# Inverting a Sinkhorn chain's sums on ScalarE (logarithm, exponential) or on VectorE (reciprocal)

## The chip, the cores and the metric

The kernel runs on one core of a Trainium2 chip. Its time is the device time of one execution in microseconds (us). An engine works through its own queue of instructions strictly in order; the queues meet through semaphores.

## The reference

Two layers work on two batches of 1024 rows of 512 numbers. The first layer is a single-head attention and, behind it, a mixing of four streams per row by a 4x4 matrix. The second layer is an attention with 32 heads, followed by a gated sum of low-rank experts. The edit lies in the mixing: the 4x4 matrix of a row comes from 50 Sinkhorn steps, each of which normalizes first the rows and then the columns.

```python
Z = logits / tau                                   # tau = 0.1
def step(carry, _):
    u, v = carry
    u = -jax.nn.logsumexp(Z + v[..., None, :], axis=-1)
    v = -jax.nn.logsumexp(Z + u[..., :, None], axis=-2)
    return ((u, v), None)
(u, v), _ = jax.lax.scan(step, (u0, v0), None, length=50)
H_res = jnp.exp(Z + u[..., :, None] + v[..., None, :])
...
H_res = (1.0 - g) * I + g * H_res
x_mixed = jnp.einsum('btij,btjc->btic', H_res, x_streams)
```

## The kernel before

**Sinkhorn.** A batch's 1024 matrices lie as 128 partitions x 8 x 4 x 4, so one instruction works on all of them: 128 elements per partition for a matrix (tiles M, Kt, Z), 32 for the row sums (aa) or column sums (bb). All of these tiles bear the name sk in the profile. The first step is made with logarithms (L535 to L549); the other 49 are made on the exponentials: `chain_pool` for the second batch, `chain_dve` for the first. In `chain_pool` GpSimd multiplies the matrix by the inverse sums (L567, L573) and adds it up in two instructions (L568 and L569 for the rows, L574 and L575 for the columns), and VectorE inverts the 32 sums (L572, L577). So one iteration crosses between the engines four times. At iteration 25 the factors are taken into Z once (L579 and after).

**What sets the order.** The chain is a Python generator. One `next` issues half an iteration: 102 of them are spread over 116 slots of the second layer (SK0, SKN, `chain_step`). A slot is one row step of the second layer's attention; there are 512. Which instruction stands where in an engine's queue is decided at build time by a scheduler with a model of the engines' times, from the program's order and the dependences. An edit of one instruction can thus move others in the queues.

**The row step** (`row_step`) computes a block of scores on TensorE (L91 into tile s), takes the row minimum on VectorE (L292, L296), the exponential with its sum on ScalarE (L300), the inverse of the sum (L324 on VectorE, L325 on ScalarE), the upper half in 16 bits on ScalarE (L330) and the lower on VectorE (L338). The columns up to a multiple of 128 are cleared on GpSimd (L342). Then SyncE's queue issues the transpose by DMA (L343), and TensorE multiplies with the values (L373) some slots later. Heads come in groups of four, 32 slots per group; a row is finished one slot after its scores.

**The other work in these slots:** weights come in by DMA on GpSimd's queue (L715) and are split there into two halves (L97 to L99; L97 waits by hand for a step of VectorE, L338). ScalarE and VectorE evacuate products (L107, L108), VectorE adds to the result (L775). The gating of the experts runs on VectorE (L921 to L961, with L204 and L205 on ScalarE). After the chain its result Hm mixes the second batch's streams (`mix0_units`, L635 loads xr on SyncE's queue, L659 on ScalarE, L660 on GpSimd), from slot 122 on.

Of the kernel before, what the change touches and what calls it, by code (L numbers as in the profile page):

```python
# [11 lines left out]
AF = mybir.ActivationFunctionType  # L12
# [42 lines left out]
def tile_model(ctx: ExitStack, tc: tile.TileContext, out: bass.AP, a: dict):  # L55
# [3 lines left out]
    V, A, G = nc.vector, nc.scalar, nc.gpsimd  # L59
# [497 lines left out]
    def chain_pool(b, Z, M, aa, bb, over_i, over_j, f2):  # L557

        Kt = sk[b, 1].rearrange("p t (i j) -> p t i j", j=4)
        h2 = sk[b, 5].rearrange("p t (i j) -> p t i j", j=2)  # L560
        h3 = h2.rearrange("p t i j -> p t (i j)").rearrange("p t (k j) -> p t k j", k=2)
        A.activation(Kt, Z, AF.Exp)
        x = Kt
        yield
        for it in range(1, 50):
            if x is not Kt:
                G.tensor_tensor(M, Kt, over_i(bb), ALU.mult)  # L567
            G.tensor_tensor(h2, x[:, :, :, 0:2], x[:, :, :, 2:4], ALU.add)  # L568
            G.tensor_tensor(aa, h2[:, :, :, 0], h2[:, :, :, 1], ALU.add)  # L569
            x = M  # L570
            yield
            V.reciprocal(aa, aa)  # L572
            G.tensor_tensor(f2(M), f2(Kt), over_j(aa), ALU.mult)  # L573
            G.tensor_tensor(h3, x[:, :, 0:2, :], x[:, :, 2:4, :], ALU.add)  # L574
            G.tensor_tensor(bb, h3[:, :, 0, :], h3[:, :, 1, :], ALU.add)  # L575
            yield
            V.reciprocal(bb, bb)  # L577
            if it == 25:
                A.activation(aa, aa, AF.Ln)  # L579
                A.activation(bb, bb, AF.Ln)  # L580
                V.tensor_tensor(f2(Z), f2(Z), over_j(aa), ALU.add)
                V.tensor_tensor(Z, Z, over_i(bb), ALU.add)
                A.activation(Kt, Z, AF.Exp)
                x = Kt
        V.tensor_tensor(M, M, over_i(bb), ALU.mult)
# [643 lines left out]
```

## Time and profile before

| what | value |
|---|---|
| time, median of 3 runs | 1848.05 us (1846.22 to 1849.40) |
| the profiled execution's own time | 1850.09 us |
| its span | 1848.3 us |
| mean granted clock of TensorE | 0.973 of full speed |
| TensorE busy, share of the span | 1710.0 us, 93% |
| VectorE | 1475.5 us, 80% |
| ScalarE | 1189.3 us, 64% |
| GpSimd | 868.0 us, 47% |
| the chain's stretch (first L568 to last L577) | 276.3 to 593.2 us |

The page names the engines PE (matmul) and PEld (weight load) for TensorE, DVE for VectorE, ACT for ScalarE, POOL for GpSimd and SP for SyncE; SPq and POOLq are instructions that issue DMAs. L572 is line 572 of the kernel. A line of waits reads: engine, tile and line that waited, behind the arrow the engine, tile and line that ended the wait, then the total in us, how often, and the longest. A line of the timeline reads: start and duration in us, engine, line, operation, tiles and shape, count, and in brackets the idle time before it with what ended that. In a table by stretch the columns are the stretch, its length and each engine's busy time with its count of instructions, then the granted clock, the DMA engines' share and what they moved. Matmuls overlap, so that a busy TensorE is not one at its peak: in the chain of work that ended last, twelve matmuls of 512 columns take 2.59 us, 0.216 us each, while the page's mean of one is 0.380.

### The profile page before, as it was taken

What the parts mean: (1) busy time and instruction counts of PE and PEld (TensorE: products, weight loads), DVE (VectorE), ACT (ScalarE), POOL (GpSimd) and SP (SyncE); (2) the same over time, 40 slices, a digit from 0 to 9 for tenths busy, and PEclk for the clock granted to TensorE, in tenths of its full rate; (3) what the DMA queues carried; (4) which work ended last, traced back from release to release, by engine and by line L of the source; (5) the groups of instructions that cost most, each with busy time, mean ns of one, the idle gap of its engine ahead of it and who ended that gap; (6) DMA issues with size and microseconds to landing.
All of it is one profiled execution on the core that took longest, in us unless ns stands there. A gap on an engine that the chain in (4) does not pass through costs nothing. (4 is left out here: it accounts for less than half of the span.)

```text
span 1848.3 us, 35002 instructions
## 1 busy us (share of the span) xinstructions
PE 1710.0 (93%) x11394; PEld 1040.1 (56%) x11394; DVE 1475.5 (80%) x4170; ACT 1189.3 (64%) x2917; POOL 868.0 (47%) x1460
## 2 busy tenths in 40 slices
PE   4767399899999999998999999999999999999998
PEld 2434156555666556665565566665666666665565
DVE  7888878978888878777577777799787877778676
ACT  3848666656676777876366666667566767666564
POOL 5568639766867455656244242334142423235200
PEclk9888699999999999999999999999999999999999
DMA  7435216666566656476383655557565655666455
GB/s 212 83 55 131 60 44 140 139 107 139 120 139 114 137 125 141 103 149 139 71 170 96 128 123 132 101 137 164 146 142 119 141 125 132 128 143 127 103 118 117
DMA packets 685033, 228.14 MB, mean 123 GB/s; under 512 B 665633, under 2 KB 665761, under 8 KB 684850
## 3 DMA queue, kind: packets, MB, share of 16 engines
q1 hardware_dynamic: 669394, 178.65, 47.1%
q0 software_dynamic: 13152, 43.07, 8.2%
q10 hardware_dynamic: 2304, 4.20, 0.7%
q8 instruction: 89, 1.46, 0.3%
q14 instruction: 94, 0.77, 0.1%
HBM read 52.81 MB, written 4.19 MB: 31 GB/s over the span
## 5 line engine op out<-in xcount | busy, mean ns | idle before, releaser
L300 ACT ACTIVATE P<-P,nm 128x1024 f32<-128x1024 f32 (+31 forms) x528 | 391.4, 742 | 279.9 <-DVE nm L292 256.0
L338 DVE SCALAR_TENSOR_TENSOR Phl<-P,r,Phl 128x64 f16<-128x64 f32 (+16 forms) x627 | 461.1, 760 | 77.6 <-ACT Phl L330 71.4
L91 PE MATMUL s<-K,Q 128*128 128x512 f16 (+22 forms) x2400 | 441.2, 317 | 19.0 <-DVE P L296 11.2
L373 PE MATMUL av<-PT,V 128*128 128x256 f16 x3456 | 427.6, 275 | 13.1 <-DMA PT<-Phl 11.0
L373 PEld LDWEIGHTS <-V 128*128 128x128 f16 x3456 | 339.3, 99 | 97.1 <-issue 11.6
L330 ACT ACTIVATE Phl<-P,r 128x1024 f16<-128x1024 f32 (+31 forms) x515 | 369.7, 731 | 17.1 <-DMA PT<-Phl 2.9
L91 PE MATMUL pp<-wo,ao 128*128 128x512 f16 x1536 | 369.3, 380 | 5.6 <-ACT ao L107 3.1
L91 PE MATMUL pp<-big,wq 128*128 128x512 f16 x1536 | 368.6, 380 | 2.0 <-DVE Q L108 1.9
L97 POOL TENSOR_SCALAR f2k<-f2k 128x512 f32<-128x512 f32 x164 | 111.2, 679 | 520.0 <-DVE Phl L338 467.7
L91 PEld LDWEIGHTS <-Q 128*128 128x128 f16 x2400 | 224.1, 98 | 177.4 <-issue 28.5
L91 PEld LDWEIGHTS <-wq 128*128 128x128 f16 x1536 | 148.8, 98 | 167.9 <-DVE Q L108 2.4
L91 PEld LDWEIGHTS <-ao 128*128 128x128 f16 x1536 | 149.7, 98 | 161.9 <-ACT ao L107 4.9
L91 PEld LDWEIGHTS <-big 128*128 128x128 f16 x1824 | 121.2, 100 | 86.4 <-DMA big<-wo 40.7
L292 DVE CUSTOM_DVE_ANT_0 P<-s,mask,nm 128x272 f32<-128x272 f32 (+15 forms) x256 | 157.7, 617 | 11.3 <-PE s L91 3.0
L296 DVE TENSOR_SCALAR_CACHE_REDUCE P<-s 128x512 f32<-128x512 f32 (+15 forms) x272 | 152.6, 563 | 10.7 <-PE s L91 9.3
L325 ACT ACTIVATE r<-r 128x1 f32<-128x1 f32 x528 | 95.9, 193 | 76.7 <-DVE r L324 76.1
L324 DVE RECIPROCAL r<-r 128x1 f32<-128x1 f32 x528 | 79.9, 156 | 81.5 <-ACT P L300 78.2
L342 POOL MEMSET Phl<- 128x192 f16 (+1 forms) x320 | 56.3, 188 | 162.6 <-DMA PT<-Phl 99.3
L107 ACT ACTIVATE ao<-av 128x512 f16<-128x512 f32 x128 | 75.0, 586 | 87.4 <-PE av L373 84.0
L292 DVE CUSTOM_DVE_ANT_0 P<-s,mask 128x32 f32<-128x32 f32 (+15 forms) x256 | 104.6, 430 | 19.2 <-PE s L91 18.9
L91 PE MATMUL pp<-big,big 128*128 128x128 f16 (+2 forms) x816 | 103.9, 283 | 16.8 <-DVE sk L604 12.7
L775 DVE SCALAR_TENSOR_TENSOR acc<-pp,acc 128x512 f32<-128x512 f32 x128 | 87.2, 681 | 36.7 <-PE pp L91 36.3
(257 smaller groups left out, 2064.2 us busy)
## 6 DMA issues: line engine op xcount, KB each, us to landing
f2k<-in_Wq POOLq DMA_DIRECT2D x64, 256.0 KB, 3.2
f2k<-in_WoT POOLq DMA_DIRECT2D x64, 256.0 KB, 3.2
PT<-Phl SPq DMA_TRANSPOSE x528, 3.3
acc<-in_x SPq DMA_DIRECT2D x16, 256.0 KB, 5.2
f2k<-in_Wup POOLq DMA_DIRECT2D x16, 256.0 KB, 3.3
xr<-V SPq DMA_DIRECT2D x32, 128.0 KB, 2.3
out<-acc ACTq DMA_DIRECT2D x16, 256.0 KB, 3.0
xr<-in_x SPq DMA_DIRECT2D x12, 256.0 KB, 3.6
```

The lines of the kernel that those rows point to most:

```text
L91: nc.tensor.matmul(dst, lhs(l), rhs(r), start=(i == 0 and j == 0), stop=(i == n - 1 and j == 2))
L97: first = G.tensor_scalar(stage, stage, scale, 1.0, ALU.mult, ALU.mult)
L107: A.activation(hl_hi, src, AF.Copy, scale=scale)
L292: last_row[0] = V.tensor_tensor_reduce(Pm[:, o:o + w], pt[:, :w], mask[:, 512 - w:], -scale, first, ALU.add, ALU.min, nm[:, k:k + 1])
L296: last_row[0] = V.tensor_scalar(Pm[:, o:o + w], pt[:, :w], -scale, first, ALU.mult, ALU.min, accum_out=nm[:, k:k + 1])
L300: A.activation(Pm[:, :W], Pm[:, :W], AF.Exp, bias=last, scale=-1.0, accum_out=r[:, 0:1])
L324: V.reciprocal(r[:, 1:2], r[:, 0:1])
L325: A.activation(r[:, 1:2], r[:, 1:2], AF.Copy, scale=PSCALE)
L330: A.activation(hl[1], Pm[:, :W], AF.Copy, scale=r[:, 1:2])
L338: last_low[0] = V.scalar_tensor_tensor(lo, Pm[:, a0:a1], r[:, 1:2], hi[:, a0:a1], ALU.mult, ALU.subtract)
L373: nc.tensor.matmul(p, v, pt, start=(k == 0), stop=(k == len(todo) - 1))
L775: V.scalar_tensor_tensor(acc[b, t], p, 1.0 / 256.0, acc[b, t], ALU.mult, ALU.add)
```

## The change

The two calls of the reciprocal in `chain_pool` become calls of a helper. Up to iteration 45 it takes the logarithm of the sums in place on ScalarE and then the exponential of its negative; from iteration 46 on it is the reciprocal on VectorE as before. `chain_dve` is not touched.

```diff
         A.activation(Kt, Z, AF.Exp)
         x = Kt
+
+        def inverse(s):
+            if it < 46:
+                A.activation(s, s, AF.Ln)
+                A.activation(s, s, AF.Exp, scale=-1.0)
+            else:
+                V.reciprocal(s, s)
+
         yield
         for it in range(1, 50):
@@
-            V.reciprocal(aa, aa)
+            inverse(aa)
             G.tensor_tensor(f2(M), f2(Kt), over_j(aa), ALU.mult)
@@
-            V.reciprocal(bb, bb)
+            inverse(bb)
```

In the changed kernel the lines behind the helper stand 8 lower: its logarithm is L559, its exponential L560, its reciprocal L562.

## The prediction

> **What bounds the kernel now.** I read the page's first and second parts, then the busy table of the stretch in which the edited code runs, then the waits of TensorE in that stretch, then those of GpSimd, and last the instructions of the tile sk.
>
> The second batch's Sinkhorn chain (tile sk, L567 to L577) runs from 276 to 593 us of a span of 1848.3 us. Beside it TensorE works on the first groups of layer 1's attention. Busy time there, in two pieces:
>
> ```profile
> core 0: us, PE busy (x) PEld busy (x) DVE busy (x) ACT busy (x) POOL busy (x), PEclk, DMA share, GB/s
> 276.00:376.00 100.00, 89.92 (x661) 55.88 (x660) 89.80 (x257) 60.59 (x151) 81.74 (x148) 0.96 0.69 139
> 376.00:593.00 217.00, 215.84 (x1439) 133.26 (x1438) 180.82 (x517) 141.56 (x348) 157.40 (x362) 0.99 0.60 124
> ```
>
> TensorE stands still for 10.1 us of the first 100 us and for 1.2 us of the 217 after. So nothing can be won after 376, only lost; what can be won lies before. VectorE is 90% busy in the first piece, ScalarE 61%. What ended TensorE's pauses between 276 and 593:
>
> ```profile
> PE av L373 <- DMA PT<-Phl: 5.5, 1, 5.5
> PE s L91 <- DVE P L296: 2.6, 1, 2.6
> PE av L373 <- DVE ao L108: 1.3, 1, 1.3
> PE pp L91 <- ACT ao L107: 1.2, 1, 1.2
> PE s L91 <- DVE nm L292: 0.6, 1, 0.6
> ```
>
> Three of five end with VectorE (4.5 us together), and the largest ends with a DMA that VectorE feeds. Next, who keeps GpSimd waiting in the same stretch, and the edited instructions beside the nearest logarithm:
>
> ```profile
> POOL sk L567 <- DVE sk L577: 20.3, 27, 2.0
> POOL f2k L97 <- DVE Phl L338: 19.5, 12, 5.7
> POOL sk L573 <- DVE sk L572: 16.2, 23, 2.8
> ```
> ```profile
> L572 DVE RECIPROCAL sk<-sk x49: 327/347/354, 277.9 to 591.6; 128x32 f32<-128x32 f32 x49
> L577 DVE RECIPROCAL sk<-sk x49: 326/349/355, 286.3 to 593.2; 128x32 f32<-128x32 f32 x49
> L542 ACT ACTIVATE sk<-sk x2: 213/221/229, 43.4 to 269.4; 128x32 f32<-128x32 f32 x2
> ```
>
> GpSimd asks for an inverse 98 times and pauses for many of the answers; with the pauses behind L324 (4.6 and 3.9 us) and L207 (0.8) they make 45.8 us.
>
> **What the change takes away.** 90 of the 98 reciprocals (iterations 1 to 45, two each) leave VectorE: 90 x 0.347 = 31.2 us. VectorE's own pauses for GpSimd in front of them (L572 8.3 us, L577 7.2 us) go too, but for the last four iterations.
>
> What that is worth is read from where TensorE stands still. Between the pauses at 276, 291.9, 339.7, 357.4 and 373.2 us the trace has 2, 10, 5 and 5 reciprocals, or 0.66, 3.46, 1.69 and 1.70 us. Against the pauses: of 1.30 us (ao, L108) 0.66 goes; of 2.60 us (P, L296) all; of 0.60 us (nm, L292) all. Sum **3.9 us**. From below, nothing goes if what VectorE waits for is late next: the rows that L338 needs come from ScalarE.
>
> The largest pause needs its own reading. TensorE's queue in front of it, SyncE's queue, and the landing times of the transposes between 358 and 374:
>
> ```profile
> 361.36 2.78 PE L373 MATMUL av<-PT,V 128*128 128x256 f16 x24
> ...
> 373.15 5.26 PE L373 MATMUL av<-PT,V 128*128 128x256 f16 x24 [5.46 <-DMA PT<-Phl]
> ```
> ```profile
> 363.17 0.33 SPq L635 DMA_DIRECT2D xr<-in_x  x1
> 364.52 2.24 SPq L343 DMA_TRANSPOSE PT<-Phl  x1
> ```
> ```profile
> DMA to landing us min/median/max: 2.8/6.1/8.6
> ```
>
> The transpose issued at 364.52 lands 8.6 us later, just ahead of TensorE's start at 373.15; over the chain's stretch the median landing is 3.4 us. It goes out right behind the 256 KB load of xr (L635), which had waited 2.1 us for VectorE's gating step L934. After the pause the same 24 matmuls take 5.26 us where the earlier 24 took 2.78, at a granted clock of 0.50 between 372 and 376: 2.48 us more. So this place costs 5.46 + 2.48 = 7.94 us. In the instruction order that the changed kernel is built with, the gating comes earlier on VectorE (its last L934 stands ahead of the lower half of the 992-wide row, not behind it) and xr's load stands one transpose earlier on SyncE. That takes the load out of the way of the late transpose. From above 7.94 us, from below nothing, since the loads of Wq on GpSimd's queue crowd the same moment. I take half, **4.0 us**.
>
> **What it adds.** 180 ScalarE instructions on 128x32. Logarithm: the row above, 0.22 us. An exponential of that shape is not in the trace; it lies between the copy of 128x1 (L325, 0.193) and the exponential of 128x128 (L540, 0.293 to 0.309), nearest the logarithm: 0.22. Sum 90 x 0.44 = 39.6 us on ScalarE, 202.2 us busy of 317 before, 241.8 after (76%). That fits beside its work: ScalarE's longest idle times there are waits for VectorE (L300 for nm, 71.6 us), which get shorter.
>
> The gating's Ln and Exp (L204, L205) run at 1207.60 and 1207.84 us for 0.21 each with nothing between them, and the one table load of the trace is at L110; in the changed order there is again one. The Trainium skill ("ScalarE: Activation LUTs", What ACT_TABLE_LOAD costs) puts a switch to another set of functions at 2.66 us, which would make 180 x 2.66 = 479 us if the two functions lay apart; its section on table sets names one set with both, and the trace agrees.
>
> The cost that can reach TensorE is GpSimd's. It sits 0.47 us between its two instructions when VectorE answers at once (0.35 of it the reciprocal). On ScalarE that is 0.47 - 0.35 + 0.22 + 0.09 (the gap between L325 and a dependent L330) + 0.22 = 0.65, so 0.18 more; x 90 = **16 us** at the least. In the changed order 43 of the 90 exponentials have another ScalarE instruction between them and their logarithm, mostly L300 or L330 (means 0.742 and 0.731 us): 43 x 0.74 = 32 more, **48 us** at the most. How long the request lies in the queue changes little: VectorE began 0.78 us (aa) and 0.41 us (bb) after the sum on average, and ScalarE begins L325 0.59 us after the L324 it waits for (all from start times in the timeline).
>
> Of the whole answer time before (49 x 1.44 + 47 x 1.02 = 118 us) 45.8 us, 39%, stood as idle time on GpSimd; the rest lay beside its other work. So 6 to 19 us more idle time, middle 12.5. It meets 19.5 us of slack, the waits of L97 for VectorE, but these lie at 12 places. What is queued behind a waiting GpSimd is the clearing of pad columns (L342), for which SyncE's transposes wait, and behind these TensorE's L373. There the order leaves room: a row is finished in the next slot, slot 4c+2 for the later row of a pair, its product is due in slot 4c+5, a slot is some 3.1 us (1572 us for 512), so 9.2 less 3.4 for the landing, nearly 6 us. I let a quarter of the middle through: **3.1 us**.
>
> Behind a waiting logarithm stand ScalarE's exponentials (L300) and evacuations (L107); VectorE paused 15.5 us for the same sums, and ScalarE has 75 us left, so I cost that at nothing; with the slack gone it is 15.5 us.
>
> The chain's end moves by some three rows in the changed order (about 10 us). The next to need it is mix0 (L659), first at 624 us, 31 us behind the chain's end: covered. From about 690 us on TensorE's order is the same in both kernels.
>
> GpSimd's L574 takes 318 ns by the median and 1204 at the longest, the long ones beside VectorE's L338. The Trainium skill ("SBUF — State Buffer", Who interferes with whom) says that a VectorE instruction with two SBUF inputs blocks a GpSimd instruction that reads SBUF, and that one with a single input in the plain mode doesn't. A reciprocal has one, so by this rule its leaving frees nothing there; the sum has no such gain either.
>
> **Sum.** The profiled execution took 1850.09 us (span 1848.3 and 1.79 around it). -3.9 - 4.0 + 3.1 = -4.8, so 1845.3. The median of the three runs shown, 1848.05, is 2.04 lower; on that footing **1843.3**, I write 1843.
>
> **Rivals.**
> - *The pauses only move.* The late transpose stays late (the Wq loads crowd it) and ScalarE's added work eats the rest: -3.9 + 3.1 = -0.8, 1847. For it: the DMA share is 0.69 there already. Against: the load of xr does move. 0.21.
> - *Slower: GpSimd becomes the bound.* The 48 us fall on it whole. It is busy 239 us of 317, pauses 46, issues 32 fetches at 0.59 us (19 us): only the 19.5 us are left. 48 - 19.5 - 6 (room of the transposes) = 22 us, less the 3.9 that VectorE gives: 1848 + 18 = 1866. It decides once GpSimd idles (19.5 + 6) / 90 = 0.28 us more per inverse, against 0.14 in the forecast. Half of that excess makes 1857. For it: GpSimd's order is strict and SyncE's transposes already wait for GpSimd in some 75 places. Against: the changed order puts other work between. 0.32.
> - *It doesn't do what it says:* table loads between the two functions, at the trace's 1.28 us a load 180 x 1.28 = 231 us. Excluded by the one load in the built order; 0.01.
> - *Forecast*, both gains in some measure: 1836 (all 11.8 us of the early pauses, nothing lost) to 1844. 0.46.
>
> **How the numbers follow.** 0.2% is 3.7 us, about what a measurement of this kernel can tell from no change. The forecast's case gives faster, the first rival same, the second and third slower: 0.46, 0.21, 0.33. The range leaves out little below (1834, a further 2 us of pauses behind 640 us) and the slower rival's far part: up to 1861.
>
> **What would show it.** Right: VectorE's busy time between 276 and 593 falls by some 31 us, ScalarE's rises by some 40; TensorE's pauses at 340 and 373 us shrink; L97's waits shrink. Wrong: pauses of TensorE (L373 for PT) after 376 us; GpSimd's waits for the exponential well over 58 us in all; TensorE's matmul of layer 1 at the same place of its order later from 420 us on.

## The result and the profile after

The changed kernel takes 1856.72 us (median of 6, 1855.54 to 1859.63) where the kernel before took 1848.17 in runs beside it: a ratio of 1.0038, 95% interval 1.002 to 1.0056. It is slower: the medians lie 8.6 us apart, and the ratio on record, which is not the quotient of the two medians, makes it some 7 us. On another chip the same kernel came out at 1.0014 (1.0003 to 1.0026). Both intervals lie above 1, so the sign is firm; the size is not. The profiled execution took 1855.54 us, span 1853.8, at a granted clock of 0.972 (before: 0.973), 5.5 us more than the one before.

In the profile of the changed kernel the logarithm is L567, the exponential L568 and the helper's reciprocal L570 (not the numbers that stand under the diff above). Lines behind the helper are 8 higher than before: GpSimd multiplies in L575 and L581 and sums in L576, L577 (rows) and L582, L583 (columns).

First the instructions of the tile sk in the changed kernel (shortest, median and longest in ns, then when):

```profile
L567 ACT ACTIVATE sk<-sk x90: 212/229/231, 279.6 to 594.1; 128x32 f32<-128x32 f32 x90
L568 ACT ACTIVATE sk<-sk x90: 212/229/231, 281.0 to 594.3; 128x32 f32<-128x32 f32 x90
```

The change does what it says, at the price that was estimated (0.22 us each). The eight reciprocals that stay on VectorE follow until 611.0 us, 18 later than the chain's last one before. Busy time by stretch, the changed kernel; the second stretch reaches to 603 us here:

```profile
core 0: us, PE busy (x) PEld busy (x) DVE busy (x) ACT busy (x) POOL busy (x), PEclk, DMA share, GB/s
276.00:376.00 100.00, 92.56 (x677) 57.30 (x675) 88.36 (x240) 66.25 (x189) 77.97 (x138) 0.95 0.67 136
376.00:603.00 227.00, 220.75 (x1461) 135.48 (x1459) 165.45 (x449) 164.71 (x500) 159.68 (x365) 0.99 0.58 121
```

The second stretch of the kernel before, to the same moment:

```profile
376.00:603.00 227.00, 225.84 (x1503) 139.58 (x1502) 188.24 (x541) 147.07 (x359) 160.44 (x368) 1.00 0.58 121
```

The kernel before has 278.0 us of VectorE and 207.7 of ScalarE in the same 327 us, this one 253.8 and 231.0. VectorE is relieved by 24 us and ScalarE takes on 23: less than the durations say (31 and 40), because neighbours on an engine overlap. In the fence on place 3 below, the exponential of 0.23 us at 453.00 is followed by an instruction that starts 0.13 later.

Now the waits between 276 and 600 us, of GpSimd, ScalarE and VectorE in the changed kernel, and behind them those of ScalarE and VectorE before:

```profile
POOL sk L581 <- ACT sk L568: 31.5, 28, 3.1
POOL sk L575 <- ACT sk L568: 28.5, 27, 2.9
POOL f2k L97 <- DVE Phl L338: 10.8, 8, 2.2
```
```profile
ACT sk L567 <- POOL sk L583: 28.0, 27, 2.3
ACT P L300 <- DVE nm L292: 26.9, 25, 6.5
ACT sk L567 <- POOL sk L577: 16.0, 19, 2.2
```
```profile
DVE r L324 <- ACT P L300: 25.2, 36, 1.8
DVE Phl L338 <- ACT Phl L330: 15.1, 23, 2.1
```
```profile
ACT P L300 <- DVE nm L292: 75.5, 51, 4.7
```
```profile
DVE r L324 <- ACT P L300: 9.6, 18, 1.0
DVE Phl L338 <- ACT Phl L330: 8.4, 15, 1.2
DVE sk L572 <- POOL sk L569: 8.3, 15, 1.8
DVE sk L577 <- POOL sk L575: 7.4, 15, 0.8
```

GpSimd waits 60.0 us for ScalarE's inverses, and 3.0 more for VectorE's last eight by the chain's end, where it waited 45.8 in all. ScalarE now waits 44.0 us for GpSimd's sums, and 48.6 us less than before for the row minimum (75.5 there). VectorE is rid of its own 15.7 us of waits for the sums, but waits 40.3 us for ScalarE's exponential and upper half where it waited 18.0. So 24 us of work and 15.7 us of waits left VectorE, and 22.3 us of waits for ScalarE came back.

TensorE's three longest pauses between 276 and 600 us, in the changed kernel's timeline:

```profile
296.16 2.08 PE L373 MATMUL av<-PT,V 128*128 128x256 f16 x9 [4.27 <-DVE ao L108]
...
457.66 0.62 PE L91 MATMUL s<-K,Q 128*128 128x160 f16 x6 [1.92 <-DVE nm L292]
469.69 4.06 PE L373 MATMUL av<-PT,V 128*128 128x256 f16 x24 [3.00 <-DMA PT<-Phl]
```

The first was 1.30 us before; the last two were not there, though before TensorE paused 1.16 us for ao (L107) at 459.1. The 2.60 us at 340 have shrunk to 0.27, the 5.46 us at 373 are gone, the 0.60 us at 357 are 0.71, and 1.58 us for ao (L107) are new at 361.7.

To see where the time moved, compare the start of each row's exponential (L300, in the timeline of ScalarE) with that of the same row in the profile before. From the first row of the stretch to the last of the kernel the difference is made of five parts:

| rows (time before) | difference gained or lost | what lies there |
|---|---|---|
| up to row 24 (274 us) | +0.6 | ahead of the edited work |
| 24 to 32 (to 294 us), **place 1** | +3.7 | the pause of 4.27 |
| 56 to 64 (371 to 401 us), **place 2** | -7.2 | the late transpose, gone |
| 80 to 168 (459 to 710 us), **place 3** | +6.3 | the pauses of 1.92 and 3.00, and slower matmuls behind |
| the other rows | +2.1 | small waits for L107 (in all 3.4 us, 1.2 before) |

The sum is +5.5, what the span shows. From 710 us on the two kernels keep their distance within about 1 us (+5.1 there, +5.5 at the end). The parts are not pauses alone: between the two rows of place 3 TensorE stands still 2.98 us before and 6.09 after, which is half of the 6.3. The other half is time in which it is busy; its granted clock between 376 and 603 us is 0.99 where it was 1.00.

### The profile page after: what moved, and what is told of

The parts are those of the page before. It is cut to its first block, busy times and chain, and to the rows that moved or that the text cites. A ratio compares the mean times of both kernels' runs of the same rounds, so it can differ in the third digit from the quotient of the medians.

```text
span 1853.8 us, 35062 instructions
## 1 busy us (share of the span) xinstructions
PE 1711.5 (92%) x11394; PEld 1039.0 (56%) x11394; DVE 1451.8 (78%) x4080; ACT 1214.9 (66%) x3097; POOL 871.6 (47%) x1460
## 5 line engine op out<-in xcount | busy, mean ns | idle before, releaser
L300 ACT ACTIVATE P<-P,nm 128x1024 f32<-128x1024 f32 (+31 forms) x528 | 391.0, 741 | 236.3 <-DVE nm L292 222.8
L338 DVE SCALAR_TENSOR_TENSOR Phl<-P,r,Phl 128x64 f16<-128x64 f32 (+16 forms) x627 | 458.7, 756 | 93.6 <-ACT Phl L330 78.6
L373 PE MATMUL av<-PT,V 128*128 128x256 f16 x3456 | 428.2, 276 | 16.2 <-DMA PT<-Phl 10.8
L373 PEld LDWEIGHTS <-V 128*128 128x128 f16 x3456 | 339.1, 99 | 100.0 <-DMA PT<-Phl 12.9
L97 POOL TENSOR_SCALAR f2k<-f2k 128x512 f32<-128x512 f32 x164 | 110.8, 677 | 501.7 <-DVE Phl L338 448.2
L292 DVE CUSTOM_DVE_ANT_0 P<-s,mask,nm 128x272 f32<-128x272 f32 (+15 forms) x256 | 158.3, 619 | 9.3 <-PE s L91 1.0
L324 DVE RECIPROCAL r<-r 128x1 f32<-128x1 f32 x528 | 80.5, 157 | 96.2 <-ACT P L300 93.1
L325 ACT ACTIVATE r<-r 128x1 f32<-128x1 f32 x528 | 96.1, 192 | 59.7 <-DVE r L324 57.4
L107 ACT ACTIVATE ao<-av 128x512 f16<-128x512 f32 x128 | 75.0, 586 | 81.4 <-PE av L373 78.1
L292 DVE CUSTOM_DVE_ANT_0 P<-s,mask 128x32 f32<-128x32 f32 (+15 forms) x256 | 104.4, 431 | 23.7 <-PE s L91 23.3
L91 PE MATMUL pp<-big,big 128*128 128x128 f16 (+2 forms) x816 | 103.8, 282 | 17.2 <-DMA big<-wo 16.7
```

The costliest lines, as they stand in the source:

```text
L91: nc.tensor.matmul(dst, lhs(l), rhs(r), start=(i == 0 and j == 0), stop=(i == n - 1 and j == 2))
L97: first = G.tensor_scalar(stage, stage, scale, 1.0, ALU.mult, ALU.mult)
L107: A.activation(hl_hi, src, AF.Copy, scale=scale)
L292: last_row[0] = V.tensor_tensor_reduce(Pm[:, o:o + w], pt[:, :w], mask[:, 512 - w:], -scale, first, ALU.add, ALU.min, nm[:, k:k + 1])
L300: A.activation(Pm[:, :W], Pm[:, :W], AF.Exp, bias=last, scale=-1.0, accum_out=r[:, 0:1])
L324: V.reciprocal(r[:, 1:2], r[:, 0:1])
```

## The experiments

**Theory:** the change's cost is made at a few places where an engine that works strictly in order stands still for another, not evenly over 90 inversions. **Rivals:** each inversion costs alike; or ScalarE's added load costs; or what counts is only that the build makes another order. Each run is compared with the kernel before on the same chip (1850.9 to 1851.5 us there). The table has every run; the differences at the places are taken as above, from one profiled execution each. Executions of one kernel scatter: those of place go from 1850.6 to 1858.2 us, and up to row 24, ahead of the edited work, the profiled ones differ from that of the kernel before by -2.4 to +3.2 us. The parts at the places repeat better (place 1 is 0.0 or +3.7 in 13 of the 16 runs), but each is one execution, while the medians come from all (12 of a kernel in most cases, 6 of skip112).

| run | ScalarE inverts in iterations | place 1 | place 2 | place 3 | median us | ratio (95% interval) |
|---|---|---|---|---|---|---|
| after_again | 1-45 (the change) | +3.7 | -7.2 | +6.5 | 1854.90 | 1.0014 (1.0003 to 1.0026) |
| none | nobody, 1-45 | +5.5 | -8.3 | +2.3 | 1850.80 | 0.9998 (0.9985 to 1.0011) |
| dummy | none | 0.0 | -0.4 | +0.1 | 1852.75 | 1.0015 (1.0001 to 1.0028) |
| load | none | +1.2 | -5.8 | +0.3 | 1848.62 | 0.9988 (0.998 to 0.9997) |
| wait | none | +0.1 | -5.8 | +4.8 | 1854.17 | 1.0014 (1.0001 to 1.0026) |
| mid | 4-19 | 0.0 | -7.0 | +1.7 | 1850.08 | 0.9992 (0.998 to 1.0004) |
| from4 | 4-45 | 0.0 | -7.0 | +3.6 | 1852.19 | 1.0005 (0.9995 to 1.0016) |
| hole | 1-19, 26-45 | +3.7 | -7.2 | +3.7 | 1853.62 | 1.0009 (0.9997 to 1.0021) |
| place | 20-25 | +3.7 | -1.0 | +4.5 | 1853.13 | 1.0014 (1.0002 to 1.0026) |
| skip | 4-19, 26-45 | 0.0 | -7.0 | 0.0 | 1842.70 | **0.9957 (0.9944 to 0.997)** |
| before120 | none, 120 slots | 0.0 | 0.0 | -0.2 | 1849.21 | 0.9992 (0.9979 to 1.0005) |
| after120 | 1-45, 120 slots | +3.7 | -7.2 | +3.2 | 1852.39 | 0.9999 (0.9989 to 1.0009) |
| before112 | none, 112 slots | 0.0 | -0.2 | +1.8 | 1852.22 | 1.0005 (0.999 to 1.0021) |
| after112 | 1-45, 112 slots | +3.7 | -7.2 | +6.9 | 1856.20 | 1.0022 (1.001 to 1.0034) |
| skip112 | 4-19, 26-45, 112 slots | 0.0 | -7.0 | 0.0 | 1839.75 | **0.9947 (0.9928 to 0.9967)** |
| skip120 | 4-19, 26-45, 120 slots | 0.0 | -7.0 | +2.4 | 1847.53 | 0.9983 (0.9972 to 0.9994) |

### What is VectorE's relief worth, and what ScalarE's load

**none** leaves out the inversion in iterations 1 to 45, so that VectorE is relieved and nobody else is loaded (its mixing matrix is then another). The row half of the edit; the column half is alike:

```diff
-            V.reciprocal(aa, aa)
-            G.tensor_tensor(f2(M), f2(Kt), over_j(aa), ALU.mult)
+            if it >= 46:
+                V.reciprocal(aa, aa)
+            G.tensor_tensor(f2(M), f2(Kt), over_j(one if it < 46 else aa), ALU.mult)
```

> The first 45 iterations are left unscaled: GpSimd multiplies by a tile of ones and nobody inverts, so the computed mixing matrix is another. VectorE loses the same 90 reciprocals as in the change, ScalarE gains nothing, and GpSimd waits for nobody. Theory 'queues' (in the change ScalarE's queue stands behind GpSimd's sums and GpSimd behind ScalarE's answer): both waits are gone, so 1838 to 1845 us, below the kernel before. Theory 'load' (the 40 us of added work on ScalarE are what costs): the same 1838 to 1845. Theory 'order' (the rebuilt order of the queues costs by local collisions, whatever the engine): anywhere in 1842 to 1856.

Measured 0.9998, above the 1838 to 1845 us that two of the three theories gave. The relief with no wait for any inverse of these iterations left gains nothing that can be measured in this build. What it wins at place 2 it loses at places 1 (+5.5, where TensorE pauses 3.5 us for ao) and 3. That is the result of one order and no bound on what relief is worth: skip, below, gains 0.4% with fewer inversions taken from VectorE.

**dummy** keeps the reciprocals and adds the 90 pairs on a tile of ones that nobody reads; **load** adds the same pairs, but orders each behind the row step that was issued last:

```diff
+        def inverse(s):
+            V.reciprocal(s, s)
+            if it < 46:
+                behind(A.activation(d, d, AF.Ln), last_low[0])
+                behind(A.activation(d, d, AF.Exp, scale=-1.0), last_low[0])
```

> The kernel before, with the 90 pairs of logarithm and exponential added on ScalarE on a scratch tile of ones that nobody waits for and that waits for nobody; VectorE still inverts. Theory 'queues': no wait is added, so 1848, plus or minus 3. Theory 'load': 1855 or more, as in the change or worse since VectorE isn't relieved. Theory 'order': anywhere in 1842 to 1856.

> The kernel before with 90 pairs of logarithm and exponential on a scratch tile, now ordered behind the row step that is being issued, so that they stand in the chain's stretch (the earlier independent pairs had been moved to 9 to 124 us and tested nothing there). They wait for nobody. Theory 'load' (ScalarE's 40 us of added work are the price): 1854 to 1860 beside 1848 to 1851 of the kernel before, a ratio of 1.003 or more. Theory 'queues' (the two-way standing of ScalarE and GpSimd is the price): a ratio of 0.999 to 1.0015. Theory 'order': anywhere from 0.998 to 1.005.

dummy failed as a test: without an order its pairs were built into the queue at 9 to 124 us, where this chain doesn't run. Its profiled execution was 2.3 us late by row 16, ahead of the stretch; after120, without such pairs, was 3.2 us late there, so this is not shown to be their cost. load has the pairs in the stretch, where ScalarE is busy 232.6 us of 327 (before 207.7, after 231.0), and takes 0.9988. So ScalarE's added load doesn't make this kernel slower. That it costs nothing, as the prediction said, is not shown: load's order loses the late transpose as well (place 2, -5.8), and between rows 24 and 56 it falls 3.7 us behind.

**wait** lets the pairs read the sums, into a scratch tile, while the reciprocal on VectorE still makes the inverse. ScalarE then waits for GpSimd's sums but nobody waits for ScalarE's answer:

```diff
+            if it < 46:
+                A.activation(d, s, AF.Ln)
+                A.activation(d, d, AF.Exp, scale=-1.0)
+            V.reciprocal(r, s)
```

> The kernel before, with the 90 pairs added on ScalarE so that each logarithm reads GpSimd's sums (into a scratch tile), while VectorE's reciprocal still makes the inverse into another tile. ScalarE's queue stands behind GpSimd as in the change, but the answer to GpSimd is as short as before and VectorE isn't relieved. Theory 'queues': 1855 to 1862 if the wait at ScalarE's head is the costly half, 1848 to 1851 if the longer answer to GpSimd is. Theory 'load': the same time as with the independent pairs. Theory 'order': anywhere.

Measured 1.0014, against 0.9988 for load with the same number of instructions: the intervals lie apart (1.0001 to 1.0026, 0.998 to 0.9997). The difference, 0.26% or some 5 us, points at the wait for the sums with the order that comes with it, but is no measure of it: the two ran on different chips, and the changed kernel itself differs by 0.24% between two chips. wait's profiled execution pauses at place 3, 1.86 us for the row minimum (nm, L292) at 456.52, as in the changed kernel, and 2.41 us for L107 at 646.50. It took 1851.30 us, though; seven of the twelve took 1854.1 to 1857.1, and what they lost no trace shows.

Both also lose the late transpose (place 2) although VectorE keeps all of its reciprocals. That gain belongs to the order that the build makes, in which xr's load no longer goes out just ahead of the late transpose (before at 363.17 us, in the changed kernel at 360.12, in load and wait behind it, at 376.43 and 374.10), and not to VectorE's relief.

### Which iterations cost

**mid** and **from4** change the condition of the helper alone, as do **hole**, **place** and **skip**:

```diff
-            if it < 46:
+            if 4 <= it < 20:                        # mid
+            if 4 <= it < 46:                        # from4
+            if it < 20 or 26 <= it < 46:            # hole
+            if 20 <= it < 26:                       # place
+            if 4 <= it < 20 or 26 <= it < 46:       # skip
```

> The change for iterations 4 to 19 alone (32 of the 90 inversions), which run from about 302 to 410 us; the rest stays on VectorE. In the changed kernel's trace TensorE loses at 296 us and from 457 to 473 us and wins 7 us at 373. If the losses belong to the places where they stand and the win to VectorE's relief in the gating stretch: 1840 to 1844 us. Theory 'queues' as an even price per inversion: 32/90 of +8.5, so 1851. Theory 'order': anywhere in 1842 to 1856.

> The change from iteration 4 on only (84 of the 90 inversions). It leaves the order of the first 25 us of the chain near that of the kernel before, where the changed kernel lost 4.3 us at 296 us beside a VectorE instruction of 3.89 us instead of 0.90. If that loss is an accident of place: 3 to 4 us below the changed kernel, a ratio of 1.001 to 1.002. Theories 'queues' and 'load' with an even price per inversion: 84/90 of the change's, 1.0035.

> The changed kernel once more, beside the next three on one chip. Its distance of 0.38% was measured with 6 runs on another chip than the variants. If it holds: a ratio of 1.003 to 1.005. If the chain's 120-slot variant and the variant from iteration 4 on (both within 0.1% of the kernel before) are the rule and the 0.38% was partly scatter between chips: 1.000 to 1.002.

> The change without iterations 20 to 25 (12 inversions back on VectorE), whose stretch, 434 to 466 us, ends in the changed kernel's pauses at 457 (1.92 us for nm) and 470 us (3.00 us for a transpose). If ScalarE's and GpSimd's standing for one another beside the widest rows is what makes these pauses: both go, 5 to 8 us below the changed kernel. If they are of the new order alone: the trace still has them, within 2 us of the changed kernel.

> The reverse: only iterations 20 to 25 are inverted on ScalarE (12 of 90), all others on VectorE. If the price sits at this place: the pauses at about 457 and 470 us appear, 4 to 8 us above the kernel before, a ratio of 1.002 to 1.004. Even price per inversion: 12/90 of the change's, 1.0005. Order: anywhere within 0.3%.

> The change without iterations 1 to 3 and 20 to 25, so without both places at which the changed kernel's trace loses (296 us, 457 to 473 us) and with the one at which it wins (7 us at 373). If the three places add up: 4 to 7 us below the kernel before, a ratio of 0.996 to 0.998. If what is won there is given back elsewhere: 0.999 to 1.001.

An even price per inversion is out: with 32 of the 90 inversions (mid) the ratio is 0.9992, with 72 (skip) 0.9957, with 84 (from4) 1.0005, with 78 (hole) 1.0009, with 12 (place) 1.0014. skip has more than twice mid's inversions on ScalarE and is faster. Without iterations 1 to 3 on ScalarE the loss of place 1 vanishes in mid, from4 and skip. skip has neither the loss of place 1 nor the pauses of place 3 and beats the kernel before by 0.4%, the changed one on the same chip by 0.6%; hole, which differs from it in iterations 1 to 3 alone, and from4, which differs in 20 to 25 alone, gain nothing. mid has the gain of place 2 and little loss at the other two; it was expected at 1840 to 1844 us and took 1850.08. Some 3 us of this it loses behind row 168, where its edit no longer runs, and this stays open.

The sum of the waits doesn't set the price. ScalarE waits almost as long for GpSimd's sums in skip, the fastest of these six, as in the changed kernel (35.8 us and 44.0 between 276 and 600 us):

```profile
ACT sk L567 <- POOL sk L577: 18.6, 19, 2.2
ACT sk L567 <- POOL sk L583: 17.2, 16, 2.2
```

hole and place contradict the simple reading that each place belongs to the iterations that run there, and missed what was expected of them. hole still has the pauses at place 3 (1.42 and 2.37 us) with VectorE inverting there. place has none at 457 or 470 us, where its inversions are on ScalarE (its +4.5 comes behind row 104), and has the pause of place 1, at which they are all on VectorE. The next two parts say why, as far as the traces tell.

### Place 1: a tie between VectorE and GpSimd

In the run place GpSimd does the same instructions in the same order as the kernel before between 284 and 298 us, and arrives there 0.9 us earlier. First GpSimd, then VectorE, in the kernel before:

```profile
287.55 1.52 POOL L477 TENSOR_TENSOR f2k<-ysum,hh 128x512 f32<-128x512 f32 x1
```
```profile
287.49 0.68 DVE L338 SCALAR_TENSOR_TENSOR Phl<-P,r,Phl 128x448 f16<-128x448 f32 x1 [0.30 <-ACT Phl L330]
...
288.69 2.52 DVE L338 SCALAR_TENSOR_TENSOR Phl<-P,r,Phl 128x480 f16<-128x480 f32 x2
```

and the same in the run place:

```profile
286.65 1.03 POOL L477 TENSOR_TENSOR f2k<-ysum,hh 128x512 f32<-128x512 f32 x1
```
```profile
286.59 1.58 DVE L338 SCALAR_TENSOR_TENSOR Phl<-P,r,Phl 128x448 f16<-128x448 f32 x1 [0.30 <-ACT Phl L330]
...
288.69 5.36 DVE L338 SCALAR_TENSOR_TENSOR Phl<-P,r,Phl 128x480 f16<-128x480 f32 x2
```

In both, VectorE's first L338 starts 0.06 us ahead of GpSimd's product L477. Before, VectorE's step keeps its 0.68 us and GpSimd's is stretched to 1.52; in the run place GpSimd keeps 1.03 and VectorE's is stretched to 1.58. From there on the loser keeps losing: the next two steps of VectorE take 5.36 us instead of 2.52, while GpSimd's L481 behind them takes 1.27 instead of 1.59. The lead of 0.9 us is gone and VectorE's evacuation ao (L108), for which TensorE waits, is 2.8 us late: 3.7 in all. In the changed kernel the pair takes 4.71 us beside another order on GpSimd (L99, L481 and L477, of two inputs each, follow one another from 290.56 to 294.1 with only a clearing between), and in after112, after120 and hole the pause is as long (+3.7 each). What decided the tie the rows do not show: the starts in the trace are as far apart in the one as in the other. It may even fall differently from one execution to the next: of place's twelve, seven took 1850.6 to 1853.4 us and five 1856.4 to 1858.2, and the profiled one, 1857.86, is of the five. Only that one was profiled, so this is not shown.

The Trainium skill ("SBUF — State Buffer", Who interferes with whom) says that a VectorE instruction with two inputs in SBUF contends with a GpSimd instruction that reads SBUF, and that issue order decides who blocks. L338 has two such inputs, and the traces agree in that each side is seen stretched, by 0.5 us (GpSimd) and 0.9 us (VectorE) at the first meeting. On the order they don't decide: VectorE starts first in both traces and is the one stretched in one of them. The prediction used that rule only to say that a reciprocal's leaving frees nothing; it did not ask what a shift of a few tenths of a us makes of the next meeting.

### Place 3: a logarithm in front of the row that is late

Near 450 us one group of heads ends with its widest rows (992 and 1024 columns) and the next starts with 32. VectorE finishes the row of 992 (L338) and only then takes the minima of the new group, for which TensorE waits. ScalarE's queue there in the changed kernel:

```profile
452.73 0.23 ACT L567 ACTIVATE sk<-sk 128x32 f32<-128x32 f32 x1 [2.18 <-POOL sk L577]
453.00 0.23 ACT L568 ACTIVATE sk<-sk 128x32 f32<-128x32 f32 x1
453.13 1.11 ACT L300 ACTIVATE P<-P,nm 128x992 f32<-128x992 f32 x1
...
454.74 0.23 ACT L568 ACTIVATE sk<-sk 128x32 f32<-128x32 f32 x1
454.87 0.19 ACT L325 ACTIVATE r<-r 128x1 f32<-128x1 f32 x1
```

and VectorE beside it:

```profile
452.31 0.08 DVE L292 DVE_READ_ACCUMULATOR2_ANT nm<- 128x1 f32 x1
...
456.25 1.25 DVE L338 SCALAR_TENSOR_TENSOR Phl<-P,r,Phl 128x992 f16<-128x992 f32 x1 [1.00 <-ACT Phl L330]
457.42 0.18 DVE L292 CUSTOM_DVE_ANT_0 P<-s,mask 128x32 f32<-128x32 f32 x1
```

The row's minimum is there at 452.39, but the exponential starts at 453.13: it stands behind a logarithm that waited 2.18 us for GpSimd's row sum. A second pair then stands between the exponential's sum and L325 (454.52, when the inverse L324 is done, to 454.87). That is 0.74 + 0.35 = 1.1 of the 1.92 us for which TensorE stands still until 457.66, when the new group's first minimum is done. In skip VectorE inverts here, ScalarE has no pair in front of the row, and the exponential follows its minimum at once:

```profile
447.08 1.12 ACT L300 ACTIVATE P<-P,nm 128x992 f32<-128x992 f32 x1 [1.94 <-DVE nm L292]
448.57 0.20 ACT L325 ACTIVATE r<-r 128x1 f32<-128x1 f32 x1 [0.27 <-DVE r L324]
```

In hole VectorE stands in ScalarE's stead: its reciprocals wait 0.99 and 0.38 us for GpSimd's sums in front of the same row's steps, and TensorE pauses 1.42. It is the same fault on another engine; why the chain meets the rows that way in hole and not in skip the runs do not settle.

The 3.00 us pause at 469.69 is another matter. SyncE issues the transpose of the 1024-wide row at 461.68, and GpSimd's queue the fetch of 256 KB of weights right behind it:

```profile
461.68 1.67 SPq L343 DMA_TRANSPOSE PT<-Phl  x1
```
```profile
461.91 0.59 POOL L723 DMA_DIRECT2D f2k<-in_Wq  x1
```

Of this one transpose the trace says who waited for it and how long it took:

```profile
  PE av L373: 3.0, 1
...
DMA to landing us min/median/max: 8.0/8.0/8.0
```

It lands 8.0 us after its issue, which is when TensorE goes on, where the median of a transpose is 3.3: the late transpose of place 2 again, at another row. All 18 profiled executions order themselves by the distance between this transpose and the nearest fetch. Where the fetch goes out within 0.25 us of it, it takes 6.9 to 9.0 us (after, after_again, from4, hole, wait, after120, after112), and TensorE pauses for it in all of these but wait. Where the fetch follows by 1.28 us or more, it takes 3.6 to 3.7 (mid, skip, skip112, skip120, none); where the fetch went 1.3 us or more ahead, 5.5 to 6.2 (the other six). No run moves the fetch alone, so that the fetch is what makes the landing late is read from this agreement and not isolated.

### Is it only the spread?

Four kernels change the number of slots over which the chain's 102 half steps are spread:

```diff
-SK0, SKN, MX0, MXN, LN1 = 1, 116, 122, 74, 198
+SK0, SKN, MX0, MXN, LN1 = 1, 120, 122, 74, 198      # or 112
```

> The kernel before with its chain spread over 120 slots instead of 116 (one number changed): only the place of the chain's instructions in the queues moves. It shows how far a mere new order moves the time. Theory 'order': it moves by 0.2% or more in some direction. Theories 'queues' and 'load': within 0.1%, 0.999 to 1.001.

> The changed kernel with its chain spread over 120 slots instead of 116. Theory 'order': its distance to the kernel before changes by 0.2% or more. Theories 'queues' and 'load': it stays at a ratio of 1.003 to 1.005.

> The kernel before with 112 slots, the control. Theory (an order rebuilt by another spread alone moves the time by up to some 0.2%): 0.998 to 1.002, the pauses at 292, 340 and 373 us changed. Rival (the order is worth nothing by itself): 1.000 within 0.0005 and the same pauses.

> The changed kernel with 112 slots. Theory: ScalarE waits for GpSimd's sums for 40 us or more again, and the time lies between 0.998 and 1.004 by whether the exponential of a late row stands behind such a wait at the turn of the group near 455 us. Rival (the change has an even price per inversion): 1.002 to 1.004 as with 116.

> ScalarE inverts in iterations 4 to 19 and 26 to 45, VectorE in the others, and the chain's half steps are spread over 112 slots in place of 116. Theory (each place costs by who stands behind a wait for GpSimd's sums; where the chain meets the turn of a head group differently, the pauses come and go): the time lies anywhere within 0.994 to 1.001 of the kernel before, and its pauses at 280 to 480 us tell which of the places it kept. Rival (leaving out the first iterations and 20 to 25 is by itself what gains): 0.9957 again, within 0.002, with no pause of TensorE for VectorE's minimum at the turn of the group near 455 us.

> The same with 120 slots. Theory: 0.994 to 1.001, other pauses than with 116 and 112. Rival: 0.9957 again, within 0.002.

Another spread alone gives 0.9992 and 1.0005, and both intervals hold 1. The pauses belong to the kernel and not to the spread: before112 and before120 have those of before, after112 and after120 those of after (4.26 us at 296, and at place 3 1.88 and 4.01 us in after112). skip112 and skip120 have those of skip. TensorE's pauses in skip112 between 276 and 600 us, the three largest of four groups:

```profile
PE pp L91 <- ACT ao L107: 4.9, 5, 1.5
PE s L91 <- DVE P L296: 1.6, 2, 1.3
PE av L373 <- DVE ao L108: 1.3, 1, 1.3
```

Nothing waits for a transpose, and no pause is longer than 1.5 us. On one chip the change has 1.0022 (112 slots) and skip 0.9947 and 0.9983 (112 and 120), on another skip has 0.9957 (116). So skip's gain is no accident of its spread, its size lies between 0.2% and 0.5%, and the expectation that another spread would bring other pauses was wrong. What differs between 0.9947 and 0.9983 is not in these pauses (the table has +2.4 at place 3 for skip120, up to 710 us); it stays open.

## Why the prediction was wrong

It foretold 1843 us and a gain; the kernel takes 1856.7 and loses. The prediction took the pauses that TensorE had before and asked by how much each would shrink. It priced the pauses that the new order would make at 3.1 us, and these decided the sign. By its steps:

- **Three pauses that end with VectorE (-3.9): failed at one.** 2.60 us at 340 fell to 0.27 as foretold, 0.60 at 357 stayed (0.71), and 1.30 at 292 grew to 4.27. Together +0.75. The failed sentence is "of 1.30 us (ao, L108) 0.66 goes": it took the pause for a matter of how much work VectorE has, where it hangs on which of VectorE and GpSimd holds the other up. This one term missed by 3.6 us.
- **The late transpose (-4.0): right in mechanism, mis-sized.** -7.2 at place 2, near the upper bound of 7.94. load and wait show that it comes with the order.
- **GpSimd's longer waits (+3.1): the waits right, the way to TensorE not.** GpSimd's waits for inverses grew by 17.2 us to the chain's end, 0.19 us for each of 90 where 0.14 was forecast and 0.28 was called decisive; L97's waits fell from 23.0 to 10.8 between 276 and 600 us. So GpSimd did not become the bound. The step that failed is the room of the transposes, "9.2 less 3.4 for the landing, nearly 6 us": it took the median landing. The transpose for which TensorE paused 3.00 us at 469.69 went out 5.0 us ahead of its turn, in time for a landing of 3.4, and took 8.0.
- **ScalarE's waits for the sums (nothing): failed.** "Behind a waiting logarithm stand ScalarE's exponentials (L300) and evacuations (L107); VectorE paused 15.5 us for the same sums, and ScalarE has 75 us left, so I cost that at nothing". The logarithms wait 44.0 us, not 15.5. The 75 us are 317 less 241.8 of work, idle time shared out over the stretch; they are of no use to a row whose minimum is already there when the logarithm in front of it waits. The trace shows 1.1 us of such a price, at place 3; wait against load suggests more, up to some 5 us. skip shows that 35.8 us of such waits can also cost nothing that is seen.
- **The added 39.6 us of ScalarE (nothing): not contradicted.** load is not slower than the kernel before; the busy time grew by only 23.
- **The chain's end: right.** It moved by 18 us rather than 10, and no pause for mix0 follows.
- **Sum.** Foretold -3.9 - 4.0 + 3.1 + 0; found +3.7 at place 1, -7.2 at place 2, +6.3 at place 3 and +2.7 elsewhere, +5.5 in all. Neither place 1 nor place 3 alone turned the sign: from4, without the loss of place 1, stands at 1.0005, and skip, with neither, at 0.9957.

Why the new order meets these places as it does, the tie of place 1 above all, stays open. Of the rivals, "the pauses only move" came nearest in mechanism: a late transpose did stay, at another row. But it counted no new pauses. The slower one came near in time (1857 for half of its excess), by another way: GpSimd idled little more than in the forecast. Of the signs named for a wrong prediction, pauses of L373 for PT after 376 us did come; GpSimd's waits for the exponential, 60.0 us, hardly passed the 58 named.

## What to carry to other kernels

When work moves to another engine, don't weigh its busy time against that engine's idle time: list what stands behind each new wait in that engine's queue, and look at the few places where that is the work the bound engine needs next (here the turn of a group, where the widest row is late). Count the pauses that a new order can make, and not only those that it can take away; where a transfer has to arrive in time, look at how late such transfers land beside others and not at their median. Taking the work away entirely shows what one order makes of it (0.9998 here) and bounds nothing. Trying the change on parts of the loop told more: leaving out 9 of 45 iterations turned a loss of 0.1 to 0.4% into a gain of 0.2 to 0.5%.

## What the runs showed of the hardware

A meeting that the trace shows 0.06 us apart in two kernels, with the same instructions in the same order on GpSimd, came out in opposite ways, and the loser went on losing for some 5 us: VectorE's two steps took 5.36 us in one and 2.52 in the other. The same transpose of a 1024-wide row landed 3.6 to 3.7 us after its issue where a fetch of 256 KB went out 1.28 us or more behind it, and 6.9 to 9.0 where the fetch went out within 0.25 us of it. The clock is a small part of the difference: it was 0.972 after and 0.973 before over the span, with slow matmuls behind the long pauses (the 24 matmuls at 469.69 us take 4.06 us where 2.78 is usual, at a granted clock of 0.63 between 470 and 474 us).
